# A planned single-core kernel: eight transfers in the planner's count, tile 2 on GpSimd's queue, and a new order

## The chip, the core and the metric

The kernel runs on one core of one Trainium2 chip. A core has TensorE (PE, matrix products and transposes), VectorE (DVE), ScalarE (ACT), GpSimd (POOL) and SyncE (SP, which here only issues DMAs), and 16 DMA engines that all issuers share. The metric is the device time of one execution in microseconds (us). Beside it the profiler gives the span of one execution, from its first to its last instruction.

## What is computed

Two batches of 1024 tokens with D = 2048 go through a quantized product with a context matrix and then through a routed low-rank layer. The parts of the reference that matter:

```python
def fake_quant(x, scale, zp):
    q = jnp.clip(jnp.round(x / s + z), QMIN, QMAX)
    return (q - z) * s
...
q1 = fake_quant(x1, x1_scale, x1_zp)
q2 = fake_quant(x2, x2_scale, x2_zp)
return jnp.matmul(q1, q2)
...
logits = jnp.einsum('bsd,ed->bse', x, route_w)
topk_v, topk_idx = jax.lax.top_k(logits, 1)
route_weight = jax.nn.one_hot(topk_idx[..., 0], E, dtype=logits.dtype) * topk_v
h = jnp.einsum('bsd,erd->bser', x, A)
wh = route_weight[..., None] * h
out = jnp.einsum('bser,eor->bso', wh, Bw) * SCALING
...
x = x + jnp.tanh(g_xattn[0]) * _L0_xattn_ref(_layernorm(x, axis=-1), ctx_4096, ...)
x = x + jnp.tanh(g_ffn[0]) * _L0_ffn_ref(_layernorm(x, axis=-1), L0_ffn_route_w, L0_ffn_A, L0_ffn_Bw)
```

x has shape (2, 1024, 2048), the context (2, 2048, 2048); there are E = 8 experts of rank 16. All inputs are float32.

## The kernel before

**Tiles and stages.** The 2048 tokens are 16 tiles of 128 (tiles 0 to 7 are batch 0, 8 to 15 batch 1). For each tile: load x (1 MB, L539), statistics, quantize (L623 on ScalarE or L632 on VectorE) and clamp (L629, L638), turn the 128 x 2048 result so that D lies on partitions, multiply by the quantized context (L704: 4 strips of 512 columns x 16 steps of K), evict with the corrections (L725, or L733 and L738), and then the feed-forward part (`ffn`). Statistics are four VectorE passes (L559, tiles in STATV) or two ScalarE passes (L577, then L587). The turn is a DMA transpose (L650, tiles in TURN) or 16 TensorE transposes (L660) with two copies (L524; with a tile in COPYV the second one is VectorE's). A row sum of the quantized tile (L675 on VectorE for SUMV, else L677 on ScalarE) goes into the correction.

**Context.** Each strip comes in four pieces of 1 MB (`strip`, load L432; a piece in FINE comes in two halves). It is scaled on ScalarE (L439) or VectorE (L450, pieces in VQ) and clamped (L446, L457). Column sums of a strip are 16 matmuls (L482) for strips in ONES, else VectorE additions and one matmul (L508). Four buffers hold raw pieces of batch 0, two those of batch 1. The strips of one batch serve groups of tiles: 0, 1, 2 together, then 3, 4, then 5, 6, 7 together; in batch 1 tiles 8, 9 together, then one by one.

**Feed-forward.** The new x must be turned once more, in float32, and multiplied by the 136 columns of `war`. Tiles in MOVE do it without TensorE transposes (`hidden_moved`): VectorE transposes 32 x 32 blocks (L760), DMAs move the blocks across partitions, ScalarE sorts (L800), TensorE multiplies (L804, 32 records). The DMAs are either 16 direct ones of 64 KB (`move`, L778) or, for tiles in VIA, one of 1 MB to DRAM (L770) and four back (`fetch`, L783). For tiles in TWO every second group of these DMAs is issued by ScalarE instead of SyncE. The other tiles use TensorE transposes (L822) with copies (L836) and products (L828). Then come a ScalarE square for the variance (L866), routing on VectorE (L877 to L886), a transpose (pw, L898) and copy (wht, L904), four output products (po, L911) with two banks, VectorE additions (L919), and the store (L932 on GpSimd's queue; the last tile's in four pieces on SyncE, L925).

**What sets the order.** No loop does. Every instruction, or a small group, is a `Task` with an engine, a cost, a rank, the tasks that it needs, and its buffers. `Plan.walk` goes through time: an engine that is free takes the task of lowest rank that is ready and has buffers. The resulting order is then issued on each engine, in order, and is fixed; only real waits (semaphores) apply on the chip. Ranks come from the position of a tile's strip in the sequence of matmul groups, less the entries of LEAD (statistics and quantization), XLEAD (x loads; XL0 for tiles 0 to 3), CTX and CQ (context), plus those of AFTER (feed-forward), SUM and COR (row sums, column sums). A DMA in the planner takes its bytes at 370 KB per us one after the other, plus 2.5 us and a slack; the number of DMAs in flight is not limited there.

**The first microseconds.** TensorE is kept busy by warm-up products (L356). SyncE's queue holds two scalars, half of tile 0, tile 1 in four pieces, the first context piece in halves, tile 2 in two pieces, three context pieces (the last in halves), tile 3, and the second strip; ScalarE's queue holds the other half of tile 0 and two scalars. GpSimd sets constants (L257 to L268) and later takes one power per tile (L609).

Of the kernel before, what the change touches and what calls it, by code (L numbers as in the profile page):

```python
# [17 lines left out]
P = 128  # L18
# [20 lines left out]
class Task:  # L39
    __slots__ = "eng cost rank fn needs bufs nbytes alone slack start end".split()  # L40


class Plan:
# [3 lines left out]

    def __init__(self, pools, kinds, hop, dma_rate, dma_delay):
        self.pools = pools
        self.kinds = kinds  # L50
        self.hop, self.rate, self.delay = hop, dma_rate, dma_delay
        self.tasks = []

    def add(self, eng, cost, rank, fn, needs=(), bufs=(), nbytes=0, alone=False, slack=0.0):

        t = Task()
        t.eng, t.cost, t.rank, t.fn, t.nbytes = eng, cost, rank, fn, nbytes
        t.alone, t.slack = alone, slack
        t.needs, t.bufs, t.start, t.end = list(needs), list(bufs), None, None
        for b in bufs:  # L60
            b.left += 1
        self.tasks.append(t)
        return t
# [10 lines left out]
    def walk(self):  # L74
# [8 lines left out]
        for w in waiting.values():  # L83
            w.sort(key=lambda t: t.rank)
        releases = []
        order = []
        now = 0.0
# [12 lines left out]
        while any(waiting.values()):  # L100
# [6 lines left out]
            for eng, w in waiting.items():  # L107
# [6 lines left out]
                for t in w:  # L114
                    at = self.ready_at(t)
                    if at is None:
                        continue
                    if at > now:
                        nxt.append(at)
                        continue  # L120
                    if t.alone and dma > now:
                        nxt.append(dma)
                        continue
                    if room(t):
                        pick = t
                        break
# [9 lines left out]
                if pick.nbytes:  # L136
                    dma = max(dma, now) + pick.nbytes / self.rate
                    pick.end = max(pick.end, dma) + self.delay + pick.slack
                for b in pick.bufs:
                    b.left -= 1  # L140
                    b.unit_end = max(getattr(b, "unit_end", 0.0), pick.end)
                    if not b.left:
                        releases.append((b.unit_end + self.hop, b))
# [13 lines left out]
def flamingo_gated_kernel(  # L157
# [42 lines left out]

    TURN = {4, 6, 7, 8, 11, 12, 13, 14, 15}
    MOVE = {3, 4, 8, 9, 10, 11, 12, 13, 14}
    pools = {"big": 10, "q2": 4, "half": 3, "q1t": 5, "wh": 2, "wht": 2, "bn": 3, "sel": 2, "away": 2}
    kinds = {k: (k, n) for k, n in pools.items()}
    kinds |= {"x": ("big", 6), "xl": ("big", 2), "st0": ("big", 4), "st1": ("big", 2), "ff": ("big", 4)}
    kinds |= {k: ("bank", n) for k, n in (("mm", 4), ("tp", 2), ("hl", 1), ("po", 2), ("cs", 1))}
    plan = Plan(pools | {"bank": 8}, kinds, hop=0.15, dma_rate=370e3, dma_delay=2.5)

# [77 lines left out]
    for tiles in sets:  # L286
# [5 lines left out]

    LATE = {4, 5, 6, 7}
    STATV = {0, 2, 3, 5, 13, 15}
    SUMV = {5, 6, 8, 14, 15}
    COPYV = {4, 5, 7, 9, 12, 14}
    ONES = {0}
    SUM = [2.5, 8.5, 8.5, 5.5, -1, 5.5, -1, 1.5, 5.5, 2.5, 3.5, 3.5, 8.5, 2.5, 0.5, 8.5]
    LEAD = [5, 7, 3, 5, 6, 3, 5, 14, 5, 8, 8, 12, 7, 7, 3, 14]
    XLEAD = [4, 4, 4, 4, 2, 1, 1, 8, 0, 6, 2, 1, 4, 3, 2, 2]  # L300
    XL0 = {0: -101, 1: -5.2, 2: -3.1, 3: -0.4}
    AFTER = [3.2, 6.2, 0.3, 1.2, -0.8, 0.7, 5.2, 5.2, 0.7, 0.7, 4.2, 6.2, 4.2, 4.2, 1.7, 3.2]
    CTX = [3, 1, 3, 4, 5, 4, 3, 2]
    COR = [1.5, 3.5, 0.5, 0.5, -0.5, 2.5, 2.5, 0.5]
    SLACK = 4.0
    VIA = {2, 3, 4, 5, 8, 9, 10, 12}
    TWO = {1, 3, 5, 6, 9, 10, 11, 12, 13, 14, 15}
    XL = {14, 15}
    PIECES = {0: 4, 1: 4, 2: 2, 3: 1}
    SPLIT = {0, 2}  # L310
    FINE = {0, 3, 4, 5}
    VQ = {0, 2, 3, 4, 9, 13, 14, 17, 20, 21, 41}
    CQ = {4: -1.8, 5: -1.1, 0: -1.1, 11: -1.0, 9: -0.2, 3: -0.1, 7: -0.6, 8: 1.1, 2: 0.2, 6: -0.9, 10: -1.5, 1: 0.7}
    SP, ACT, DVE, PE, POOL = "SP", "ACT", "DVE", "PE", "POOL"
# [8 lines left out]
    )  # L323
    t_raw = [
        add(SP, 0.9, -101.0, lambda: load_scalars(nc.sync, (0, 1)), nbytes=1, slack=3.0),
        add(ACT, 0.9, -100.9, lambda: load_scalars(nc.scalar, (2, 3)), nbytes=1, slack=3.0),
    ]
    t_gates = add(POOL, 1.1, -101, lambda: load_scalars(nc.gpsimd, (4, 5)), nbytes=1, slack=3.0)
    t_set = add(POOL, 2.0, -100, set_up_more)
# [196 lines left out]
    def tokens(t):  # L526
# [7 lines left out]
        loads = []  # L534
        for i in range(pieces):
            loads.append(
                add(
                    ACT if early and i % 2 else SP, 0.5, XL0.get(t, rank - XLEAD[t]),
                    lambda i=i: (nc.scalar if early and i % 2 else nc.sync).dma_start(  # L539
                        xx.ap()[:, ts(i, w)], x[b, ts(m, P), ts(i, w)]  # L540
                    ),
                    [t_ctx[1, NN - 1, NQ - 1]] if t in XL else [t_ctx[0, NN - 1, 1]] if t > 3 else [], [xx], nbytes=4 * P * w, slack=SLACK if t > 3 else 0.0 if t else 1.0,
                )
            )
# [203 lines left out]
    def hidden_moved(t, xx, hl, rank):  # L748
# [24 lines left out]
        for g in range(BPC):  # L773
# [8 lines left out]
            def fetch(g=g, queue=queue):  # L782
# [7 lines left out]
                if t in VIA  # L790
                else add(on, 2.6, rank - 0.5, move, turns, [turned, across], nbytes=4 * P * NC)
            )
# [49 lines left out]
    def ffn(t):  # L842
# [7 lines left out]
        p = (hidden_moved if t in MOVE else hidden)(t, xx, hl, rank)  # L850
        junk = flat("half", f"junk_{t}", F16, D)

# [5 lines left out]
        def inverse():  # L858
# [3 lines left out]

        a = add(DVE, 0.25, rank, mean, [t_x2[t, n] for n in range(NN)])
        a = add(
            ACT, 2.2, rank + 0.3,
            lambda: nc.scalar.activation(junk.ap(), xx.ap(), AF.Square, bias=nm, accum_out=sq),  # L866
            [a], [xx, junk],
        )
        t_r2 = add(DVE, 0.3, rank, inverse, [a])
        wh = buf("wh", f"wh_{t}", [P, E, R], F32)  # L870
# [3 lines left out]
        def route():  # L874
# [17 lines left out]

        a = add(DVE, 1.5, rank - 1, route, [p, t_r2, t_set], [hl, wh, sel_b])
        pw = buf("tp", f"pw_{t}", [P, NC], F32)
        wht = buf("wht", f"wht_{t}", [ER, P], F32)
        a = add(
            PE, 0.15, rank,
            lambda: nc.tensor.transpose(  # L898
# [4 lines left out]
        d = add(  # L903
            ACT, 0.28, rank - 1, lambda: nc.scalar.copy(wht.ap(), pw.ap()[:ER, :P]), [a], [pw, wht]  # L904
        )
        done = []
        for n in range(NN):
            po = buf("po", f"po_{t}_{n}", [P, NC], F32)
            a = add(
                PE, 0.87, rank,  # L910
                lambda n=n, po=po: nc.tensor.matmul(  # L911
# [8 lines left out]

            done.append(add(DVE, 0.75, rank - 0.5, finish, [a], [po, xx]))
            if end:
                add(
                    SP, 0.6, rank,
                    lambda n=n: nc.sync.dma_start(  # L925
# [4 lines left out]
        if not end:  # L930
            add(
                POOL, 0.6, rank, lambda: nc.gpsimd.dma_start(out[b, ts(m, P), :], xx.ap()),  # L932
                done, [xx], nbytes=4 * P * D,
            )
# [56 lines left out]
```

## Time and profile before

| quantity | value |
| --- | --- |
| median of three runs | 394.18 us (392.55 to 394.59) |
| the profiled execution: its own time | 394.16 us |
| the profiled execution: span | 392.4 us |
| granted TensorE clock, mean | 0.991 |
| main matmuls, L704 | 1024 records, 234.6 us |
| output products, L911 | 128 records, 60.5 us |
| hidden products, L804 and L828 | 512 records, 63.8 us |
| transposes of the quantized tiles, L660 | 112 records, 7.6 us |
| DMA traffic | 90.07 MB, mean 230 GB/s |
| transfers issued by SyncE, ScalarE | 69.80 MB, 4.20 MB |
| transfers issued by GpSimd | 15.73 MB |

A line of a group or of the timeline names line, engine, operation, output <- input, shapes and count; the bracket or the part behind the bar is the idle time of that engine just before and what ended it. A line of the stage table gives the stretch, the busy time and count of PE, PEld (weight loads), DVE, ACT and POOL, the granted clock, the busy share of the DMA engines and the GB/s. A float32 matmul leaves two records. Ends of matmuls are modelled, so lengths of single records overlap; the chain of waits shows the real pace. Some matmul records can be missing. Idle time of an engine that is not the bound costs nothing.

### The profile page before, as it was taken

The numbers are of one execution on the slowest core, as the hardware profiler recorded it, in microseconds if no ns is written. First come the engines' busy times: TensorE is split into PE (matmuls) and PEld (weight loads), VectorE is DVE, ScalarE is ACT, GpSimd is POOL, SyncE is SP. The second block draws the span as 40 slices with busy tenths as digits, with TensorE's granted clock in tenths as the row PEclk, the third lists the DMA queues.
The fourth block names the chain that finished last, engine by engine and source line by source line (L and its number), as shares of the span: only waits on it lengthen the run. The fifth ranks groups of instructions, "written<-read, shape, count | busy, mean of one in ns | idle before, by whom it ended". The sixth has DMA issues, their size and how long they took to land.

```text
span 392.4 us, 5340 instructions
## 1 busy us (share of the span) xinstructions
PE 374.7 (96%) x1969; PEld 216.5 (55%) x1969; DVE 305.1 (78%) x711; ACT 233.0 (59%) x225; POOL 23.6 (6%) x52
## 2 busy tenths in 40 slices
PE   4689999999999999999999999999999999999994
PEld 4544445657654654654756674444646455666671
DVE  3699999997977398794699659999779777676553
ACT  1799995699624536889979895656545042402140
POOL 3010000010001000010010010001010000000000
PEclk9879999999999999999999999999999999999999
DMA  6999999805548928998798478356366727767222
GB/s 211 342 396 388 387 372 377 322 0 109 214 150 320 226 109 254 395 406 261 241 333 309 146 270 280 109 160 143 74 198 178 208 115 214 215 209 211 119 106 108
DMA packets 50658, 90.07 MB, mean 230 GB/s; under 512 B 21320, under 2 KB 23368, under 8 KB 46152
## 3 DMA queue, kind: packets, MB, share of 16 engines
q1 hardware_dynamic: 45812, 69.80, 54.3%
q0 software_dynamic: 2224, 15.73, 10.0%
q10 hardware_dynamic: 2596, 4.20, 4.7%
q8 instruction: 15, 0.25, 0.3%
q14 instruction: 11, 0.09, 0.1%
HBM read 58.79 MB, written 23.07 MB: 209 GB/s over the span
## 4 chain that ended last, share of the span: by engine, by line
PE 75%; DMA 13%; DVE 6%; ACT 2%; SPq 1%; issue 1%; ACTq 0%
PE mm L704 45%; PE po L911 12%; PE hl L804 8%; PE hl L828 6%; DMA across<-away 4%; DMA st<-in_ctx_dram 3%; DMA away<-turned 3%; PE px L822 3%; DMA across<-turned 2%; DMA x<-in_x_dram 1%; PE pq L660 1%; ACT turned L800 1%; DVE turned L760 1%; DVE x L733 1%; DVE q L450 1%
## 5 line engine op out<-in xcount | busy, mean ns | idle before, releaser
L704 PE MATMUL mm<-q,q1t 128*128 128x512 f16 x1024 | 234.6, 380 | 4.1 <-ACT q1t L524 2.7
L704 PEld LDWEIGHTS <-q1t 128*128 128x128 f16 x1024 | 100.0, 98 | 124.3 <-issue 15.6
L439 ACT ACTIVATE q<-st,raw,rs 128x2048 int16<-128x2048 f32 (+1 forms) x30 | 57.3, 1919 | 13.3 <-PE mm L704 9.0
L911 PE MATMUL po<-wb,wht 128*128 128x512 f32 x128 | 60.5, 594 | 0.4 <-ACT wht L904 0.4
L919 DVE SCALAR_TENSOR_TENSOR x<-po,th,x 128x512 f32<-128x512 f32 x64 | 47.2, 748 | 15.8 <-PE po L911 13.0
L866 ACT ACTIVATE junk<-x,mine 128x2048 f16<-128x2048 f32 x16 | 32.1, 2005 | 21.3 <-DVE mine L854 21.2
L733 DVE SCALAR_TENSOR_TENSOR x<-mm,sc,x 128x512 f32<-128x512 f32 x48 | 35.2, 744 | 10.2 <-PE mm L704 10.1
L904 ACT COPY wht<-pw 128x128 f32<-128x128 f32 x16 | 4.2, 264 | 57.6 <-PE pw L898 41.7
L623 ACT ACTIVATE q<-x,mine 128x2048 int16<-128x2048 f32 (+1 forms) x16 | 31.7, 1984 | 9.9 <-DVE mine L603 7.1
L804 PEld LDWEIGHTS hl<-war,turned 128*128 128x128 f32 x288 | 34.6, 190 | 5.0 <-ACT turned L800 2.8
L804 PE MATMUL hl<-war,turned 128*128 128x136 f32 x288 | 35.3, 280 | 1.1 <-ACT turned L800 1.1
L738 DVE SCALAR_TENSOR_TENSOR x<-x,mine,corr 128x512 f32<-128x512 f32 x48 | 35.2, 746 | 1.6 <-ACT corr L515 0.8
L911 PEld LDWEIGHTS po<-wb,wht 128*128 128x128 f32 x128 | 23.4, 190 | 19.9 <-issue 13.2
L828 PE MATMUL hl<-war,xt 128*128 128x136 f32 x224 | 28.5, 280 | 0.4 <-ACT xt L836 0.4
L828 PEld LDWEIGHTS hl<-war,xt 128*128 128x128 f32 x224 | 27.4, 190 | 1.9 <-ACT xt L836 0.9
L587 ACT ACTIVATE q<-x,mine 128x2048 f16<-128x2048 f32 x10 | 20.0, 1997 | 8.4 <-DVE mine L582 8.4
L800 ACT COPY turned<-across 128x1024 f32<-128x1024 f32 x18 | 17.9, 1041 | 9.6 <-DMA across<-away 5.6
L760 DVE STREAM_TRANSPOSE turned<-x 128x512 f32<-128x512 f32 x36 | 22.9, 683 | 0.2 <-DMA across<-away 0.2
L836 ACT COPY xt<-px 128x512 f32<-128x512 f32 x28 | 15.7, 583 | 10.7 <-PE px L822 10.7
L559 DVE BATCH_NORM_STATS2 bn<-x 128x6 f32<-128x512 f32 x24 | 15.3, 682 | 8.2 <-DMA x<-in_x_dram 8.2
L932 POOL DMA_DIRECT2D out_dram<-x x15 | 8.7, 583 | 204.5 <-DVE x L919 156.8
L677 ACT ACTIVATE q<-q 128x2048 f16<-128x2048 f16 x11 | 20.9, 1904 | 0.0
(93 smaller groups left out, 318.9 us busy)
## 6 DMA issues: line engine op xcount, KB each, us to landing
st<-in_ctx_dram SPq DMA_DIRECT2D x28, 1024.0 KB, 10.8
out_dram<-x POOLq DMA_DIRECT2D x15, 1024.0 KB, 5.0
x<-in_x_dram SPq DMA_DIRECT2D x13, 1024.0 KB, 4.8
away<-turned SPq DMA_DIRECT2D x6, 1024.0 KB, 3.9
st<-in_ctx_dram SPq DMA_DIRECT2D x8, 512.0 KB, 12.9
across<-away SPq DMA_DIRECT2D x16, 256.0 KB, 6.3
across<-away ACTq DMA_DIRECT2D x8, 256.0 KB, 6.1
x<-in_x_dram SPq DMA_DIRECT2D x6, 256.0 KB, 5.0
```

The lines of the kernel that those rows point to most:

```text
L439: nc.scalar.activation(part.bitcast(I16), st.ap().rearrange("p (k n) -> p k n", k=QK)[:, ts(h, n)], AF.Relu, bias=z2, scale=rs2,)
L623: nc.scalar.activation(qb.ap()[:, ts(h, hw)].bitcast(I16), xx.ap()[:, ts(h, hw)], AF.Relu, bias=nb, scale=a)
L704: lambda k=k: nc.tensor.matmul(acc.ap(), qt.ap()[:, k, :], qb.ap()[:, k, :], start=(k == 0), stop=(k == KC - 1)),
L733: lambda: nc.vector.scalar_tensor_tensor(xs(), acc.ap(), c, xs(), ALU.mult, ALU.add),
L738: lambda: nc.vector.scalar_tensor_tensor(xs(), xs(), rs_[t], corr[:, ts(s, NC)], ALU.add, ALU.add, accum_out=ss),
L760: nc.vector.transpose(turned.ap().rearrange("p (g k i) -> p k g i", i=BLK, k=KC)[:, ts(n, BPC)], xx.ap()[:, ts(n, NC)].rearrange("p (k g j ...
L800: nc.scalar.copy(o[:, ts(h, KC // H)], i[:, ts(h, KC // H)])
L804: nc.tensor.matmul(hl.ap()[:, : ER + E], turned.ap()[:, ts(k, P)], war[:, k, :], start=(k == 0), stop=(k == KC - 1),)
L828: nc.tensor.matmul(hl.ap()[:, : ER + E], xt.ap()[:, ts(k, P)], war[:, k, :], start=(k == 0), stop=(k == KC - 1),)
L866: lambda: nc.scalar.activation(junk.ap(), xx.ap(), AF.Square, bias=nm, accum_out=sq),
L911: lambda n=n, po=po: nc.tensor.matmul(po.ap(), wht.ap(), wb[:, ts(n, NC)], start=True, stop=True),
L919: nc.vector.scalar_tensor_tensor(xs, po.ap(), gf, xs, ALU.mult, ALU.add)
```

## The change

The planner gets a limit: with eight transfers (counted in parts, for SyncE and ScalarE together and for GpSimd apart) under way, the next waits for the eighth last to land. Tasks that issue several transfers say so. Tile 2's x load moves to GpSimd's queue (XPOOL). The second half of the feed-forward part (pw, wht, po, finish, store) gets a rank of its own, later by POR[t]. An alternative for the second variance on VectorE is added, but its set BN2 is empty. All tables of the order are replaced.

```diff
@@ Plan.walk
         releases = []
+        landed = {}
...
+                    under_way = landed.get(t.eng == "POOL", [])
+                    if t.nbytes and len(under_way) >= self.most and under_way[-self.most] > now:
+                        nxt.append(under_way[-self.most])
+                        continue
                     if room(t):
...
                     pick.end = max(pick.end, dma) + self.delay + pick.slack
+                    landed.setdefault(eng == "POOL", []).extend([pick.end] * pick.parts)
@@ flamingo_gated_kernel
-    TURN = {4, 6, 7, 8, 11, 12, 13, 14, 15}
-    MOVE = {3, 4, 8, 9, 10, 11, 12, 13, 14}
+    TURN = {4, 6, 11, 12, 13, 14, 15}
+    MOVE = {3, 4, 6, 8, 10, 11, 12, 13, 14}
...
-    plan = Plan(pools | {"bank": 8}, kinds, hop=0.15, dma_rate=370e3, dma_delay=2.5)
+    plan = Plan(pools | {"bank": 8}, kinds, hop=0.15, dma_rate=370e3, dma_delay=2.5, most=8)
...
-    LATE = {4, 5, 6, 7}
-    STATV = {0, 2, 3, 5, 13, 15}
-    SUMV = {5, 6, 8, 14, 15}
-    COPYV = {4, 5, 7, 9, 12, 14}
+    LATE = {4, 5, 6, 7, 10, 15}
+    STATV = {0, 1, 3, 5, 12, 13, 14}
+    SUMV = {2, 5, 6, 8, 12, 14}
+    COPYV = {0, 3, 4, 5, 7, 9, 14}
     ONES = {0}
-    SUM = [2.5, 8.5, 8.5, 5.5, -1, 5.5, -1, 1.5, 5.5, 2.5, 3.5, 3.5, 8.5, 2.5, 0.5, 8.5]
-    LEAD = [5, 7, 3, 5, 6, 3, 5, 14, 5, 8, 8, 12, 7, 7, 3, 14]
-    XLEAD = [4, 4, 4, 4, 2, 1, 1, 8, 0, 6, 2, 1, 4, 3, 2, 2]
-    XL0 = {0: -101, 1: -5.2, 2: -3.1, 3: -0.4}
-    AFTER = [3.2, 6.2, 0.3, 1.2, -0.8, 0.7, 5.2, 5.2, 0.7, 0.7, 4.2, 6.2, 4.2, 4.2, 1.7, 3.2]
-    CTX = [3, 1, 3, 4, 5, 4, 3, 2]
-    COR = [1.5, 3.5, 0.5, 0.5, -0.5, 2.5, 2.5, 0.5]
+    SUM = [0.5, 8.5, 2.5, 1.5, -1, 1.5, 1.5, 2.5, 5.5, 2.5, 8.5, 1.5, 8.5, 8.5, 1.5, 8.5]
+    LEAD = [6, 14, 10, 8, 6, 5, 8, 14, 5, 5, 8, 14, 4, 6, 4, 6]
+    XLEAD = [4, 4, 4, 4, 0, 4, 3, 10, 2, 10, 3, 1, 4, 2, 6, 0]
+    XL0 = {0: -101, 1: 2.2, 2: -4.0, 3: 4.4}
+    AFTER = [1.2, 6.2, 2.2, 2.2, 0.3, -0.8, 4.2, 5.2, -0.8, 3.2, 6.2, 6.2, 4.2, 1.7, 5.2, 2.2]
+    CTX = [8, 6, 5, 5, 5, 5, 4, 3]
+    COR = [2.5, 1.5, 7.5, 0.5, 1.5, 1.5, -0.5, 0.5]
     SLACK = 4.0
-    VIA = {2, 3, 4, 5, 8, 9, 10, 12}
-    TWO = {1, 3, 5, 6, 9, 10, 11, 12, 13, 14, 15}
-    XL = {14, 15}
-    PIECES = {0: 4, 1: 4, 2: 2, 3: 1}
-    SPLIT = {0, 2}
-    FINE = {0, 3, 4, 5}
-    VQ = {0, 2, 3, 4, 9, 13, 14, 17, 20, 21, 41}
-    CQ = {4: -1.8, 5: -1.1, 0: -1.1, 11: -1.0, 9: -0.2, 3: -0.1, 7: -0.6, 8: 1.1, 2: 0.2, 6: -0.9, 10: -1.5, 1: 0.7}
+    VIA = {0, 2, 3, 5, 9, 12, 14}
+    TWO = {0, 1, 4, 5, 7, 9, 11, 13, 15}
+    XL = {15}
+    PIECES = {0: 4, 1: 4, 2: 2, 3: 4}
+    SPLIT = {0}
+    FINE = {3, 6}
+    VQ = {0, 4, 5, 6, 8, 9, 15, 17, 19, 21, 27, 33, 39, 44, 51}
+    XPOOL = {2}
+    POR = [0, 0, 1.5, 1, 0, 2, 1.5, 0, 1.5, 0.5, 0, 0.5, 0, 1, 2, 1.5]
+    BN2 = set()
+    CQ = {4: -1.2, 5: -1.6, 0: 1.2, 11: -1.3, 9: -0.9, 3: 0.6, 7: 0.8, 8: -0.9, 2: 1.3, 6: -2.0, 10: -1.1, 1: 1.3}
@@ tokens
+            queue = (
+                (ACT, nc.scalar) if early and i % 2 else (POOL, nc.gpsimd) if t in XPOOL else (SP, nc.sync)
+            )
...
-                    ACT if early and i % 2 else SP, 0.5, XL0.get(t, rank - XLEAD[t]),
+                    queue[0], 0.5, XL0.get(t, rank - XLEAD[t]),
@@ hidden_moved
-                else add(on, 2.6, rank - 0.5, move, turns, [turned, across], nbytes=4 * P * NC)
+                else add(on, 2.4, rank - 0.5, move, turns, [turned, across], nbytes=4 * P * NC, parts=4)
@@ ffn
+        behind = rank + POR[t]
...
-            PE, 0.15, rank,
+            PE, 0.15, behind,
...
-            ACT, 0.28, rank - 1, lambda: nc.scalar.copy(wht.ap(), pw.ap()[:ER, :P]), [a], [pw, wht]
+            ACT, 0.28, behind - 1, lambda: nc.scalar.copy(wht.ap(), pw.ap()[:ER, :P]), [a], [pw, wht]
...
-                PE, 0.87, rank,
+                PE, 0.87, behind,
...
-            done.append(add(DVE, 0.75, rank - 0.5, finish, [a], [po, xx]))
+            done.append(add(DVE, 0.75, behind - 0.5, finish, [a], [po, xx]))
```

Entries of VQ count twice the piece's number, plus one for a second half; odd entries of pieces that come whole have no effect, nor have entries of COPYV for tiles in TURN or of VIA for tiles outside MOVE. LATE tiles take their corrections in one wide VectorE pass (L716) ahead of the matmuls' eviction (L725) instead of one pass per strip behind it (L738).

## The prediction

> **What bounds the kernel now.** I read the engine totals first, then the slices, then a table by stages.
>
> ```profile
> PE 374.7 (96%) x1969; PEld 216.5 (55%) x1969; DVE 305.1 (78%) x711; ACT 233.0 (59%) x225; POOL 23.6 (6%) x52
> ...
> PE   4689999999999999999999999999999999999994
> ```
>
> TensorE is the bound: in the slices it is full but for the first three and the last. The stage table (columns: stretch, busy time of each engine, granted clock, DMA share, GB/s) says how full:
>
> ```profile
> 21.00:28.50 7.50, 7.35 (x38) 3.26 (x36) 7.17 (x16) 7.50 (x8) 1.81 (x1) 0.78 1.04 400
> 28.50:62.00 33.50, 33.28 (x179) 16.16 (x180) 31.69 (x59) 32.39 (x25) 0.89 (x1) 1.00 1.06 374
> 62.00:130.00 68.00, 67.63 (x359) 39.59 (x357) 59.31 (x148) 40.34 (x45) 4.33 (x7) 1.00 0.61 210
> 130.00:200.00 70.00, 69.06 (x377) 39.23 (x375) 51.55 (x118) 53.88 (x46) 4.19 (x5) 1.00 0.81 275
> 200.00:300.00 100.00, 100.00 (x510) 54.15 (x508) 84.11 (x201) 69.22 (x66) 5.01 (x9) 1.00 0.63 198
> 300.00:373.30 73.30, 73.11 (x392) 45.86 (x391) 51.46 (x120) 15.99 (x21) 2.69 (x5) 1.00 0.60 180
> ```
>
> From 28.5 to 373.3 TensorE stands only 0.22 + 0.37 + 0.94 + 0 + 0.19 = 1.7 us. And "busy" is real there: the chain of waits has nine main matmuls in 1.94 us, 0.216 each, everywhere. So a new order can win only (a) before 28.5, (b) those 1.7 us, (c) behind 373.3; and added TensorE work costs its full time.
>
> (a) The start, TensorE's timeline first (start, length, idle before), then ScalarE's:
>
> ```profile
> 14.87 1.07 PE L660 MATMUL pq<-idh,q 128*128 128x128 f16 x16 [0.55 <-DVE q L629]
> 18.42 1.03 PE L704 MATMUL mm<-q,q1t 128*128 128x512 f16 x2 [2.48 <-ACT q1t L524]
> 20.88 1.01 PE L704 MATMUL mm<-q,q1t 128*128 128x512 f16 x2 [1.42 <-DVE q L446]
> ```
> ```profile
> 11.22 1.91 ACT L577 ACTIVATE q<-x 128x2048 f16<-128x2048 f32 x1 [1.44 <-DMA x<-in_x_dram]
> ...
> 13.13 1.23 ACT L623 ACTIVATE q<-x,mine 128x1024 int16<-128x1024 f32 x1
> 14.26 1.99 ACT L587 ACTIVATE q<-x,mine 128x2048 f16<-128x2048 f32 x1
> ...
> 16.25 1.23 ACT L439 ACTIVATE q<-st,raw,rs 128x1024 int16<-128x1024 f32 x1
> 17.38 0.99 ACT L524 COPY q1t<-pq 128x1024 f16<-128x1024 f16 x1
> ```
>
> (ScalarE's first line is tile 1's statistics, waiting for tile 1's load; tile 0's own quantization and copy stand behind it.) By 28.5 TensorE has done 12 main matmuls, 12 column sums and 16 transposes: 24 x 0.216 + 0.9 = 6.1 us of work at full clock. It had half the clock from 17.7 to 24.2. The second piece of context (1 MB) was issued at 9.65 and landed at 21.0, since tile 1 (four pieces), tile 2 and the first context piece go before it, and because the early transfers are slow:
>
> ```profile
> 1.39 5.99 SPq L539 DMA_DIRECT2D x<-in_x_dram  x6
> ```
> ```profile
> 2.00:16.00 14.00, 9.29 (x54) 8.64 (x52) 7.22 (x24) 6.47 (x7) 2.45 (x15) 1.00 0.88 280
> ...
> 16.00:30.00 14.00, 10.00 (x53) 4.59 (x54) 12.30 (x32) 11.79 (x13) 2.37 (x2) 0.76 1.04 398
> ```
>
> SyncE takes 6 us for six issues of 0.43 us, because with eight in flight it waits for landings; meanwhile 280 GB/s move, where 398 do later.
>
> (c) The end. The last tile's product runs to 382.2, then VectorE routes, and nothing is left for TensorE:
>
> ```profile
> 383.55 0.33 PE L898 MATMUL pw<-idf,wh 128*128 128x128 f32 x1 [1.37 <-DVE wh L886]
> 384.29 3.70 PE L911 MATMUL po<-wb,wht 128*128 128x512 f32 x8 [0.41 <-ACT wht L904]
> ```
>
> 1.8 us of idle; the 4.3 us behind 388.1 (last VectorE pass and store) stay.
>
> **The parts and their prices.**
>
> *Start.* By the new ranks SyncE issues tile 0, then the first strip's four context pieces (five transfers), then tile 1's four, then the second strip. Tile 2 goes by GpSimd, ready there when its constants are set (4.04); its two issues last 0.58 each, and GpSimd's next work, a 0.56 us power for tile 0, came at 9.5: no delay. Tile 2 takes tile 1's old place (its statistics now on ScalarE), tile 1 takes tile 2's (on VectorE). Context pieces 1 and 2 go into the issue slots that tile 1's four pieces had (4.2 to 7.1), so they are behind 3 MB instead of 4 and 5. At 390 GB/s from 5 us on, pieces 0 to 3 land near 12.8, 15.5, 18.2 and 21, against 21.0 for piece 1 before.
> The unknown is when tile 2 lands, as ScalarE's in-order queue should stop at its statistics before tile 0's quantization. Before shows no load on GpSimd; the nearest rows are its stores of the same 1 MB:
>
> ```profile
> out_dram<-x POOLq DMA_DIRECT2D x15, 1024.0 KB, 5.0
> ```
> ```profile
> out_dram<-x POOLq DMA_DIRECT2D x1, 1024.0 KB, 10.6
> ```
>
> 5.0 us is the median, 10.6 the store at 167.9, beside a full SyncE queue, 7.7 one beside a half-full queue. From 4.6 that is 9.6, 12.3 or 15.2. I take 12.1. Then ScalarE: 1.9 + 1.2 + 2.0 + 1.0 = 6.0 with overlap (the 1.2 us context piece in between is now VectorE's), first matmul at 18.1. From there TensorE always has work: piece 0 is ready at about 15, piece 1 at 20.9 (ScalarE 2.1, clamp 0.7), the others by 24.3, tile 2 by 26. Half clock lasts, as before, 3.3 us of steady work: 1.65 us of work by 21.4, then 7.1 by 28.5, together 8.75 against 6.1: **-2.6 us**. Landing at 9.6: first matmul near 16, starved between pieces, but at full clock: -4. Landing at 15.2: first matmul at 21.2, work 1.65 + 4.0: **+0.4**.
>
> The page "TensorE: Matmul & The Clock Gate" of the Trainium skill (HAM oscillation; PE-mode transpose) has the clock fall after about 3.4 us without matmuls and says transposes do not count as such. Here the last warm-up ended at 14.3 and the clock fell near 17.7, in spite of transposes to 15.9. By that rule a tile 2 that lands before about 11.7 keeps the clock, worth up to 1.65 us more. "DMA: Bandwidth & Descriptors" (Issuing engines are not separate DMA queues) speaks against the GpSimd load: all issuers share the 16 engines and only issue time is saved; by it the 12.1 would lean to 15.2, and the sum to +3 on mine.
>
> *Transposes.* Tiles 7 and 8 leave the DMA transpose (9 tiles to 7): 32 more transposes on a full TensorE, 16 take 0.89 us in the chain: **+1.8 us**. Moves of the hidden state stay nine (6 in, 9 out), so no change in px work; main, product and output matmuls stay.
>
> *End.* Ranks now set tile 14's output (66.2) behind tile 15's product (65.2) and before tile 15's output (66.7). Its 3.4 us cover route 15, but finishes queue behind that route on VectorE and only two output banks exist, so some 0.4 of idle stays: **-1.4 us**. That tile 15 is LATE brings its last eviction 0.75 us forward, which tile 14's product hides. (0 for the end if tile 14's move through DRAM is late: 5.6 + 7.6 + 1.05 in the chain's worst, under the 13.8 us of tile 15's matmuls and 7 of tile 13's).
>
> *VectorE and ScalarE.* One tile more of statistics (+3.0 VectorE, -4.3 ScalarE), one row sum (+2.4, -2.1), copies 2 to 5 on VectorE (+2.1; ScalarE 12 to 13, +1.0), context scalings (-0.8, +0.5), tile 2's split gone (-0.8, +0.9), tiles 10 and 15 in LATE (one pass of 2.35 us, L716, for four of 0.75 + 0.08, L738, less four reads of 0.08: -0.6 each): VectorE +4.7 to 310 of 392, ScalarE -4. I count 0, since both have room after 62 (VectorE 59 of 68, 52 of 70). If it loses this cover, up to +2; where a stall ends sooner, -1.
>
> *SyncE.* Direct moves go from three tiles to six: 24 to 72 issues there, 48 x 0.59 = 28 us more, less 3 stores and 4 fetches (2.7). Two DMA transposes that stop the queue go. Tiles 6, 8 and 10 have all 16 issues on SyncE: 9.4 us in a row, against 4.7 when shared. The way through DRAM took 13.3 us in the chain, the direct one 10, so alone on SyncE 14.7: about equal. I take 0 for the mid holes; bounds -1.7 (none left) and +6.
>
> Sum against the profiled execution (394.16; span 392.4; the median of the runs is 394.18, so the same): 394.16 - 2.6 + 1.8 - 1.4 + 0 = **392.0**.
>
> **Rivals.**
> *Given back* (394.6): tile 2 lands after 15 (break-even at 14.8), or ScalarE and VectorE, 97 and 95% busy from 28.5 to 62, cannot deliver earlier. Start 0 to +0.4, end -1.4, transposes +1.8: 394.2 to 395.0. For it: those shares; against: 2 us of idle ScalarE from 18.4 to 20.6 that work would fill.
> *SyncE late* (398, the other side): the order on TensorE is fixed, so a product whose move is late stops it. Place: L804 behind the copy L800 behind the last of 16 issues. If tiles 6, 8 and 10 come 2 us late each, +6: 394.16 - 2.6 + 1.8 - 1.4 + 6 = 398. It decides against the forecast's gain when the new holes pass 2.2 us, and gives a measurable loss past 4.1. For it: SyncE stood behind other waits at such moves for up to 9.9 us; before's 0.86 and 0.19 us at L804 are of this kind. Against: the cost in the code, 2.4 for four issues, is the measured 4 x 0.59.
> *All comes* (388.9): landing near 9.6 (-4), holes gone (-1.7), end and transposes as above: 394.16 - 4 - 1.7 - 1.4 + 1.8.
>
> **Chances.** Forecast 0.42, given back 0.20, SyncE late 0.26, all comes 0.12. A measurement tells 0.5% (392.2 and 396.2 against 394.18). The forecast lies at that edge: 0.31 faster, 0.11 same; given back 0.17 same, 0.03 slower; late 0.26 slower; all comes 0.12 faster. Faster 0.43, same 0.28, slower 0.29. Range: from just under "all comes" to "late", 388 to 398.
>
> **What would show it.** Right: second context piece landed by 16, first matmul by 18.5 with no gap over 0.5 us behind it, 144 transposes at L660, no 1.4 us gap before the last pw, idle between 28.5 and the last main matmul at most 2 us. Wrong: ScalarE idle past 13 before tile 2's L577, gaps at L804 over 1 us, or gaps at the main matmul between 30 and 62.

## The result, and the profile after

The changed kernel takes **393.58 us** (median of 22 runs, 391.98 to 395.90), the kernel before in the same comparison 394.02 (22 runs, 392.38 to 395.21). The ratio is **0.9997, interval 0.9978 to 1.0016**: no difference. The forecast was 392.0. The profiled execution after took 393.32 us, 0.84 less than the one before.

| | before | after |
| --- | --- | --- |
| profiled execution, span | 392.4 | 391.4 |
| first main matmul begins | 18.42 | 21.94 |
| TensorE idle, 28.5 to the last main matmuls | 1.7 | 0.1 |
| last output product ends | 388.0 | 384.95 |
| from there to the end of the span | 4.4 | 6.4 |

The totals, the slices and the stage table of the profile after (columns as before):

```profile
PE 375.3 (96%) x2001; PEld 219.0 (56%) x2001; DVE 307.8 (79%) x709; ACT 228.6 (58%) x219; POOL 22.9 (6%) x54
...
PE   5689999999999999999999999999999999999993
```
```profile
28.50:62.00 33.50, 33.49 (x182) 16.30 (x181) 32.52 (x60) 31.64 (x23) 0.55 (x1) 1.00 1.05 378
62.00:130.00 68.00, 68.00 (x373) 40.63 (x372) 54.42 (x133) 41.48 (x47) 3.75 (x6) 1.00 0.48 178
130.00:200.00 70.00, 69.97 (x396) 39.99 (x394) 60.14 (x125) 49.84 (x43) 3.84 (x5) 1.00 0.73 236
200.00:300.00 100.00, 99.92 (x514) 56.33 (x513) 85.64 (x206) 61.15 (x60) 6.18 (x11) 1.00 0.67 216
300.00:370.00 70.00, 70.00 (x364) 41.54 (x363) 47.72 (x116) 24.27 (x27) 2.17 (x4) 1.00 0.54 159
```

Second column less third: between 28.5 and 370 TensorE stands 0.1 us in all. In this execution the middle is full, so what was won must have been lost at one of the two ends.

The end, TensorE's timeline of after (output products are now L945, pw is L932):

```profile
377.01 0.27 PE L932 MATMUL pw<-idf,wh 128*128 128x128 f32 x1
377.70 1.98 PE L945 MATMUL po<-wb,wht 128*128 128x512 f32 x4 [0.41 <-ACT wht L938]
379.52 0.27 PE L932 MATMUL pw<-idf,wh 128*128 128x128 f32 x1
379.63 5.32 PE L945 MATMUL po<-wb,wht 128*128 128x512 f32 x12
```

The wait of 1.37 us before the last pw is gone, as foreseen; one of 0.41 is left. TensorE ends 3.0 us sooner than before, the span only 1.0. Where did 2 us go? VectorE's last pass ends 0.78 us behind the last product in both kernels (388.77 before; 381.55 + 4.18 = 385.73 after). The rest is stores. The DMA view of the last stretch (376 to 393), line by line output <- input, queue, count, KB each, median us from issue to landing; before, then after:

```profile
out_dram<-x POOLq DMA_DIRECT2D x1, 1024.0 KB, 4.1
out_dram<-x SPq DMA_DIRECT2D x4, 256.0 KB, 2.4
```
```profile
out_dram<-x POOLq DMA_DIRECT2D x1, 1024.0 KB, 4.2
out_dram<-x SPq DMA_DIRECT2D x4, 256.0 KB, 4.6
```

And the issues, GpSimd's and SyncE's timelines, before and then after:

```profile
379.12 0.53 POOL L932 DMA_DIRECT2D out_dram<-x  x1 [10.40 <-DVE x L919]
```
```profile
386.23 2.91 SPq L925 DMA_DIRECT2D out_dram<-x  x4
```
```profile
382.59 0.53 POOL L966 DMA_DIRECT2D out_dram<-x  x1 [23.27 <-DVE x L953]
```
```profile
383.18 3.85 SPq L959 DMA_DIRECT2D out_dram<-x  x4
```

Tile 14's store, 1 MB, waits for all four additions of tile 14. The new order put these right before tile 15's, so the store leaves 0.6 us before tile 15's first piece, and the four pieces need 4.6 us instead of 2.4. (Before, tile 14's store left at 379.12, 7 us before the first piece.)

The start, timelines of TensorE and ScalarE after (transposes L674, column sums L493, main matmuls L718; tile 2's statistics L591):

```profile
17.75 1.03 PE L674 MATMUL pq<-idh,q 128*128 128x128 f16 x8 [3.67 <-DVE q L643]
18.58 1.91 PE L493 MATMUL cs<-q,ones 128*128 128x512 f16 x4
```
```profile
13.19 1.91 ACT L591 ACTIVATE q<-x 128x2048 f16<-128x2048 f32 x1 [4.83 <-DMA x<-in_x_dram]
...
18.22 2.08 ACT L450 ACTIVATE q<-st,raw,rs 128x2048 int16<-128x2048 f32 x1
20.20 0.98 ACT L535 COPY q1t<-pq 128x1024 f16<-128x1024 f16 x1
```

Tile 2 landed at about 13.1, not 12.1. ScalarE then took a context piece (18.22) before tile 0's copy (20.20), which the prediction had left out, so main matmuls begin at 21.94 and not at 18.1; column sums run from 18.58. From tile 0's own transposes to 28.5 TensorE has done 12 column sums, 18 main matmuls and 16 transposes of the next tile: 30 x 0.216 + 0.9 = 7.4 us of work, against 6.1 before and the 8.75 that were forecast (both counted in the same way).

### The profile page after: what moved, and what is told of

Same layout as the page of the kernel before. It is cut to its first block, busy times and chain, and to the rows that moved or that the text cites. A ratio compares the mean times of both kernels' runs of the same rounds, so it can differ in the third digit from the quotient of the medians.

```text
span 391.4 us, 5431 instructions
## 1 busy us (share of the span) xinstructions
PE 375.3 (96%) x2001; PEld 219.0 (56%) x2001; DVE 307.8 (79%) x709; ACT 228.6 (58%) x219; POOL 22.9 (6%) x54
## 4 chain that ended last, share of the span: by engine, by line
PE 91%; ACT 3%; DMA 2%; issue 1%; POOL 1%; DVE 0%; POOLq 0%; ACTq 0%
PE mm L718 56%; PE po L945 14%; PE hl L818 9%; PE hl L842 7%; PE px L836 3%; DMA x<-in_x_dram 2%; PE pq L674 2%; ACT q L637 1%; ACT q L450 1%; ACT q L601 1%; ACT q1t L535 1%; ACT q L691 0%; PE pw L932 0%; PE cs L519 0%; POOL row L265 0%
## 5 line engine op out<-in xcount | busy, mean ns | idle before, releaser
L718 PE MATMUL mm<-q,q1t 128*128 128x512 f16 x1024 | 233.3, 379 | 0.7 <-ACT q1t L535 0.7
L718 PEld LDWEIGHTS <-q1t 128*128 128x128 f16 x1024 | 99.8, 98 | 119.1 <-issue 10.9
L945 PE MATMUL po<-wb,wht 128*128 128x512 f32 x128 | 60.6, 595 | 0.4 <-ACT wht L938 0.4
L637 ACT ACTIVATE q<-x,mine 128x2048 int16<-128x2048 f32 (+1 forms) x16 | 32.6, 2040 | 24.2 <-DVE mine L617 14.8
L818 PEld LDWEIGHTS hl<-war,turned 128*128 128x128 f32 x288 | 34.8, 190 | 2.7 <-issue 1.1
L818 PE MATMUL hl<-war,turned 128*128 128x136 f32 x288 | 35.3, 280 | 0.1
L945 PEld LDWEIGHTS po<-wb,wht 128*128 128x128 f32 x128 | 23.4, 190 | 21.3 <-issue 14.9
L747 DVE SCALAR_TENSOR_TENSOR x<-mm,sc,x 128x512 f32<-128x512 f32 x40 | 29.4, 744 | 4.1 <-PE mm L718 3.7
L752 DVE SCALAR_TENSOR_TENSOR x<-x,mine,corr 128x512 f32<-128x512 f32 x40 | 29.4, 746 | 1.1 <-DVE x L747 0.5
L739 DVE SCALAR_TENSOR_TENSOR x<-mm,sc,x 128x512 f32<-128x512 f32 x24 | 17.6, 746 | 12.4 <-PE mm L718 12.3
L691 ACT ACTIVATE q<-q 128x2048 f16<-128x2048 f16 x10 | 19.1, 1907 | 9.1 <-DMA q1t<-q 9.1
L774 DVE STREAM_TRANSPOSE turned<-x 128x512 f32<-128x512 f32 x36 | 24.1, 693 | 0.0
L457 DVE TENSOR_SCALAR q<-q 128x2048 f16<-128x2048 int16 (+1 forms) x29 | 19.1, 662 | 3.5 <-ACT q L450 3.5
L573 DVE BATCH_NORM_STATS2 bn<-x 128x6 f32<-128x512 f32 x28 | 17.9, 681 | 4.8 <-DMA x<-in_x_dram 4.8
```

The costliest lines, as they stand in the source:

```text
L457: nc.vector.tensor_scalar(part, part.bitcast(I16), QMAX, MID, ALU.min, ALU.subtract)
L637: nc.scalar.activation(qb.ap()[:, ts(h, hw)].bitcast(I16), xx.ap()[:, ts(h, hw)], AF.Relu, bias=nb, scale=a)
L718: lambda k=k: nc.tensor.matmul(acc.ap(), qt.ap()[:, k, :], qb.ap()[:, k, :], start=(k == 0), stop=(k == KC - 1)),
L747: lambda: nc.vector.scalar_tensor_tensor(xs(), acc.ap(), c, xs(), ALU.mult, ALU.add),
L752: lambda: nc.vector.scalar_tensor_tensor(xs(), xs(), rs_[t], corr[:, ts(s, NC)], ALU.add, ALU.add, accum_out=ss),
L774: nc.vector.transpose(turned.ap().rearrange("p (g k i) -> p k g i", i=BLK, k=KC)[:, ts(n, BPC)], xx.ap()[:, ts(n, NC)].rearrange("p (k g j ...
```

## The experiments

Ratios are to the kernel before, run beside each kernel on the same chip, with 95% intervals. "Span" is that of the profiled execution. The groups e1 to e4, e5 to e8, e9 to e12 and e13 to e15 ran at different times, not all on one chip; medians are best compared within a group, ratios across groups.

| run | what | median | ratio | span |
| --- | --- | --- | --- | --- |
| e1_strips | after, tile 14's store in four | 391.43 | 0.9967 (0.9933 to 1.0001) | 388.7 |
| e2_tile2_sync | after, tile 2 by SyncE | 393.30 | 1.0008 (0.9984 to 1.0032) | 390.4 |
| e3_both | e1 and e2 | 390.42 | 0.9944 (0.9914 to 0.9973) | 388.7 |
| e4_por14 | after, tile 14's output early again | 392.74 | 1.0007 (0.9978 to 1.0035) | 391.8 |
| e5_no_limit | after, no count of transfers | 404.95 | 1.0268 (1.0230 to 1.0306) | 400.9 |
| e6_before_limit | before, planner counts eight | 403.46 | 1.0239 (1.0191 to 1.0287) | 402.2 |
| e7_turn78 | after, tiles 7, 8 by DMA transpose | 393.59 | 1.0014 (0.9984 to 1.0045) | 391.3 |
| e8_before_por | before, tile 14's output late | 392.63 | 0.9971 (0.9952 to 0.9991) | 390.9 |
| e9_after | after again | 394.19 | 1.0015 (0.9989 to 1.0041) | 393.9 |
| e10_both | e3 again | 391.57 | 0.9935 (0.9920 to 0.9949) | 390.6 |
| e11_before_por_strips | e8, store in four | 390.74 | 0.9921 (0.9907 to 0.9935) | 388.7 |
| e12_quant0_first | e3, tile 0's quantize first | 391.32 | 0.9939 (0.9916 to 0.9961) | 389.2 |
| e13_after_swap | after, a load behind tile 3's move | 393.57 | 1.0009 (0.9988 to 1.0030) | 391.8 |
| e14_both_swap | e3 with e13 | 391.93 | 0.9953 (0.9932 to 0.9974) | 390.1 |
| e15_before_end_again | e11 again | 391.18 | 0.9949 (0.9927 to 0.9970) | 389.4 |

**The end: is it the store?** e1 splits tile 14's store; each piece goes as soon as its addition is done.

```diff
-        if not end:
+        if t == NT - 2:
+            for n in range(NN):
+                add(
+                    POOL, 0.6, behind,
+                    lambda n=n: nc.gpsimd.dma_start(
+                        out[b, ts(m, P), ts(n, NC)], xx.ap()[:, ts(n, NC)]
+                    ),
+                    [done[n]], [xx], nbytes=4 * P * NC,
+                )
+        elif not end:
...
```

> The changed kernel with tile 14's store in four pieces of 256 KB, each behind its own addition, in place of one of 1 MB behind all four; everything else stands in the same order. Store theory (tile 14's 1 MB store, issued at 382.6, shares the DMA engines with tile 15's four pieces, which land in 4.6 us instead of 2.4): the pieces of tile 14 start near 379.6, tile 15's pieces land in about 2.5 us again, and from the last output product to the end of the span it is 4.4 us as in the kernel before, not 6.4: about -2.0 us, 391.5. Rival (the end is longer for another reason, such as the order of the last additions): the distance stays near 6.4 us and the time near 393.5.

The DMA view of e1's last stretch:

```profile
out_dram<-x POOLq DMA_DIRECT2D x4, 256.0 KB, 2.7
out_dram<-x SPq DMA_DIRECT2D x4, 256.0 KB, 2.9
```

The last pieces land in 2.9 us, and the span ends 4.7 us behind the last output product (388.7 - 384.0), not 6.4: of the 2.0 us, about 1.8 come back. That the collision of stores costs them is shown in the profile. In the runs' times e1 alone is not told from the kernel before (its interval reaches 1.0001); e10 below, beside e9, is.

e4 undoes the other half: `POR[14]` from 2 to 0, so tile 14's output no longer goes between tile 15's product and tile 15's output.

> The changed kernel with POR[14] at 0 instead of 2: tile 14's output products go before tile 15's hidden product again, and nothing covers the last routing. Store theory: the idle of TensorE before the last pw comes back (about 1.4 to 1.8 us), but tile 14's store is out some 3.5 us earlier and tile 15's pieces land in 2.4 us again (-2.1): together 0 to -0.7 us against the changed kernel. Rival (only TensorE's idle counts): +1.4 us or more, 395.

TensorE's timeline of e4, then its DMA view of the last stretch:

```profile
382.91 0.30 PE L932 MATMUL pw<-idf,wh 128*128 128x128 f32 x1 [1.46 <-DVE wh L919]
383.62 3.70 PE L945 MATMUL po<-wb,wht 128*128 128x512 f32 x8 [0.41 <-ACT wht L938]
```
```profile
out_dram<-x SPq DMA_DIRECT2D x4, 256.0 KB, 2.5
```

The idle time is back and the collision is gone; the time is that of after. So in the changed kernel the edit at the end moves 1.4 us from TensorE to the stores, and by itself is worth nothing.

e8 puts this edit alone into the kernel before, e11 adds the split store.

```diff
+    POR = {14: 5.8, 15: 0.5}
...
+        behind = rank + POR.get(t, 0)
...
```

As in the changed kernel, `behind` is then the rank of pw, copy, po, additions and store.

> The kernel before with the second half of tiles 14 and 15 apart (POR 5.8 and 0.5: tile 14's output behind tile 15's hidden product, as in the changed kernel); the order is otherwise the old one. Store theory: TensorE's idle before the last pw goes (-1.4 to -1.8 us at the last output product), but tile 14's 1 MB store meets tile 15's pieces, the way from the last output product to the end grows from 4.4 to about 6.4 us, so in sum 0 to +0.6 us against the kernel before. Rival (TensorE's idle alone counts): -1.4 us or more, and 4.4 us stay.

> The kernel before with tile 14's output behind tile 15's hidden product (as e8) and tile 14's store in four pieces; nothing else of the change. Store theory: TensorE's idle at the end goes and the stores do not collide: -1.8 us from the idle, 4.4 us behind the last output product, so about 391.6, and that is what the changed kernel would have had from its ranks apart alone. Rival (the end of the old order has no room for it): 393 or more.

Tile 14's hidden product, the same point of the order in all three, on TensorE's timelines of before, e8 and e11:

```profile
366.93 3.87 PE L804 MATMUL hl<-war,turned 128*128 128x136 f32 x32
```
```profile
365.55 3.87 PE L805 MATMUL hl<-war,turned 128*128 128x136 f32 x32
```
```profile
365.04 3.87 PE L805 MATMUL hl<-war,turned 128*128 128x136 f32 x32
```

From there to the end of the span: 392.4 - 366.93 = 25.47 before, 390.9 - 365.55 = 25.35 in e8, 388.7 - 365.04 = 23.66 in e11. At the end, then, the edit alone is worth 0.1 and with the split 1.8, as the theory has it. The stores agree: in e8 tile 15's pieces need 4.5 us and the span ends 6.4 behind the last output product, in e11 2.9 and 4.7. Yet the spans are 1.5 and 3.7 shorter: the other 1.4 and 1.9 us lie ahead of that point, where the instructions and their order are the same as before. Most of it, 0.9 and 1.1 us, is there already at the first hidden product (76.56 before, 75.67 and 75.46): the wait of 1.42 us for scaled context near 20.9, which the profile before has, is in neither. The kernel before itself ran from 392.38 to 395.21, so one profiled execution of each cannot say more; in the medians beside them e8 is 0.9 us and e11 3.2 us under the kernel before. Why e8 gains at all in its runs stays open. e15 repeated e11:

> The kernel of e11 once more, beside these: the kernel before, with the new end and the store in four pieces alone. By its terms 1.8 us under the kernel before; if the first measurement holds, 3.2 us under it (near 390.7).

391.18, 0.9949: a gain of 0.3 to 0.7%, a little smaller than in e11; by the medians 1.9 us, near the 1.8 that the end explains. The kernel before with its end mended is thus as good as the whole change with the end mended (e3, e10), and both beat both kernels.

**The start.** e2 takes tile 2 back to SyncE, the planned order untouched.

```diff
-                (ACT, nc.scalar) if early and i % 2 else (POOL, nc.gpsimd) if t in XPOOL else (SP, nc.sync)
+                (ACT, nc.scalar) if early and i % 2 else (POOL, nc.sync) if t in XPOOL else (SP, nc.sync)
```

> The changed kernel with the two pieces of tile 2's load issued by SyncE, at the same place of the order, in place of GpSimd; no other instruction moves. Theory (on GpSimd's queue tile 2 shares the engines with context pieces 0 and 1, lands at 13.1, and ScalarE stands 4.8 us before its statistics): on SyncE it stands ahead of the context, lands near 9.5, ScalarE starts L591 there, tile 0's second half of transposes comes near 14 instead of 17.8, and the first main matmul near 18.5 instead of 21.9; context pieces 0 to 3 land about as before, as the bytes ahead of them are the same. If TensorE is the bound from there on, -2 us or more at the last output product. Rival 1 (the context sets the start): first products earlier, but waits for pieces 1 to 3 take it back, 0 to -0.5 us. Rival 2 (GpSimd's queue is a gain, since SyncE's eight are taken): tile 2's pieces fill SyncE's eight, context piece 0 goes out after 5 instead of 4.0, later pieces up to 1 us later, 0 to +1 us.

> Both edits of this set, tile 14's store in four pieces and tile 2 on SyncE. If store theory and queue theory are both right, they add up, since one is at each end of the span: -4 us against the changed kernel, near 389.5. If only one is right, near 391.5; if neither, near 393.5.

ScalarE's timeline of e2:

```profile
11.56 1.91 ACT L591 ACTIVATE q<-x 128x2048 f16<-128x2048 f32 x1 [3.09 <-DMA x<-in_x_dram]
```

Tile 2 comes 1.6 us sooner than by GpSimd's queue, and the last output product ends 0.9 us sooner in the profile; in the runs' times the difference is not told from nothing. With both edits (e3) the median is 390.42, between the 389.5 expected if both theories held and the 391.5 if one did. e12 asks whether ScalarE's order around tile 2 matters: in e3's order, tile 0's quantization and clamp of the first half go before tile 2's statistics.

> The kernel of e10 with one move in the fixed order: ScalarE quantizes tile 0's first half, and VectorE clamps it, before tile 2's statistics, not behind them. Theory (tile 0's turn waits for tile 2's landing through ScalarE's queue): TensorE's wait of 2.7 us before the second half of tile 0's transposes goes, the first column sums start up to 0.8 us earlier, and the end comes 0.3 to 0.8 us earlier. Rival (the start is set by context piece 1 behind ScalarE's full queue): that wait goes, but TensorE waits as much longer before the second column sums, and the time stays.

TensorE's timeline of e12 (transposes are L676 there):

```profile
12.61 1.06 PE L676 MATMUL pq<-idh,q 128*128 128x128 f16 x16
15.75 1.02 PE L493 MATMUL cs<-q,ones 128*128 128x512 f16 x4 [2.08 <-DVE q L468]
18.93 1.87 PE L493 MATMUL cs<-q,ones 128*128 128x512 f16 x4 [2.16 <-DVE q L457]
```

The wait inside tile 0's transposes (4.05 us in e10, the same kernel without this move, and 2.70 in e3) is gone, and two waits of 2.1 us for scaled context stand in its place; the time stays (391.32 beside e10's 391.57). Tile 2 was not what the start depends on: context pieces behind ScalarE's and VectorE's full queues are.

**The transposes.** e7 gives tiles 7 and 8 back to the DMA transpose (`TURN = {4, 6, 7, 8, 11, ...}`); the planner orders anew.

> The changed kernel with tiles 7 and 8 in TURN again: DMA transposes in place of 32 TensorE transposes and four copies; the plan is the same up to the middle of the first batch, then worked out anew. Price theory (added TensorE work costs its full time): TensorE's work falls by 32 x 0.056 = 1.8 us and the last output product ends 1.8 us earlier, unless the two DMA transposes, which want no other transfer ahead of them, open holes on TensorE; idle between 28.5 and 370 then shows how much, and I expect 0.5 to 1 us, so -0.8 to -1.3. Rival (the transposes stood in idle time of TensorE anyway): 0. Rival (the DMA transposes stop SyncE's queue): idle over 2 us, +0.5 us or more.

Its stage table:

```profile
62.00:130.00 68.00, 67.70 (x359) 39.91 (x358) 56.70 (x134) 39.85 (x45) 3.31 (x6) 1.00 0.57 195
130.00:200.00 70.00, 69.50 (x384) 39.77 (x383) 59.90 (x132) 52.28 (x44) 4.39 (x6) 1.00 0.76 239
...
300.00:370.00 70.00, 69.05 (x355) 40.42 (x354) 48.14 (x119) 24.55 (x25) 2.16 (x4) 1.00 0.53 158
```

1.8 us less work, and 0.30 + 0.50 + 0.95 = 1.75 us of idle back; after had 0.1. TensorE's waits of e7 from 28.5 on (total, times, longest):

```profile
PE po L945 <- ACT wht L938: 1.1, 3, 0.4
PE pw L932 <- DVE wh L919: 0.5, 1, 0.5
PE hl L818 <- ACT turned L814: 0.5, 1, 0.5
```

None of them ends at a DMA transpose: 0.4 of the first line is the wait at the very end that after has too, the rest are waits for routing, for its copy and for a moved hidden state. So work and idle time balance here, but that the DMA transposes themselves made the holes is not shown: the planner ordered everything behind them anew, and the wait at L818 comes and goes without them too (see the spread, below).

**The planner's count.** e5 lifts it (`most=10000`) with the new tables; e6 puts the count (with `parts` and 2.4 for 2.6) into the planner of before with the old tables.

> The changed kernel with its new tables, planned without the limit of eight (most=10000), so that the order is worked out anew under the old belief; GpSimd's load and the second half's ranks stay. The changed kernel has 0.1 us of idle on TensorE between 28.5 and 370, the kernel before 1.7. Limit theory (the holes are gone because the planner now knows that transfers wait for the eighth last): idle between 28.5 and 370 comes back to 1.5 us or more, and the time to 395 or more. Rival (the tables were searched with that planner, and any other plan from them is worse for no reason of its own): idle of 3 us or more, not at waits for DMAs alone. Rival (the limit matters little): under 0.7 us, time within 1 us of the changed kernel's 393.6.

> The kernel before with its old tables, planned with the limit of eight, parts counted and the direct move at 2.4; nothing else of the change. Limit theory: the idle of TensorE between 28.5 and 370 falls from 1.7 to under 0.7 us, -1 us or more against the kernel before. Rival (old tables fit the old planner): the new order has more idle than 1.7 us, and the time is 395 or more.

Stage tables of e5, then of e6:

```profile
28.50:62.00 33.50, 29.39 (x165) 14.80 (x164) 30.34 (x57) 33.34 (x24) 1.09 (x2) 0.95 1.06 378
```
```profile
130.00:200.00 70.00, 66.51 (x363) 38.81 (x361) 48.56 (x110) 42.72 (x36) 2.82 (x5) 0.98 0.71 219
200.00:300.00 100.00, 96.70 (x501) 53.78 (x500) 83.78 (x195) 70.43 (x66) 5.80 (x9) 1.00 0.78 235
```

Each crossing is 2.4 to 2.7% slower (four runs each), in different places: 4.1 us of idle in one wait near the start in e5, with 3.3 us more at two moved hidden products, and 6.8 in the middle in e6. So the count by itself does not remove holes; as far as these two runs show, each set of tables fits the planner with which it was searched.

**The spread.** Half of after's 22 runs lie from 391.98 to 393.42, half from 393.73 to 395.90; the kernel before spreads nearly as widely (392.38 to 395.21). e9 looks again.

> The changed kernel once more, beside the next three on one chip, so that they can be compared with it: 393.3 to 393.9.

> The changed kernel with tile 14's store in four pieces and tile 2 on SyncE (as e3), with more rounds. Store theory: -2.0 us against the changed kernel from the store, and what tile 2's earlier landing gives, 0 to -1: 390.5 to 391.5. Rival (the first measurement was a lucky draw of starts): 392.5 or more.

e10's six runs lie from 390.50 to 392.40; the slowest is its profiled execution, with a hole of 1.81 us at L818. e9's 12 runs lie at 392.17 to 393.45 and 394.93 to 396.92; its profiled execution took 395.72. TensorE's and SyncE's timelines of e9, each followed by the same stretch of after:

```profile
137.67 5.64 PE L818 MATMUL hl<-war,turned 128*128 128x136 f32 x32 [1.89 <-ACT turned L814]
```
```profile
136.51 3.97 PE L818 MATMUL hl<-war,turned 128*128 128x136 f32 x32
```
```profile
118.73 0.34 SPq L553 DMA_DIRECT2D x<-in_x_dram  x1
119.96 0.33 SPq L784 DMA_DIRECT2D away<-turned  x1
```
```profile
118.55 0.34 SPq L553 DMA_DIRECT2D x<-in_x_dram  x1
120.66 0.33 SPq L784 DMA_DIRECT2D away<-turned  x1
126.60 2.57 SPq L797 DMA_DIRECT2D across<-away  x4
```

In e9 tile 3's way to DRAM (L784) starts 1.23 us behind a load of 1 MB instead of 2.1, and lands in 8.3 us instead of 5.8; the hidden product then waits 1.89 us and runs 1.67 us longer, together some 3.5. Eight traces have the load ahead of the move, and they line up: where it left 1.8 to 2.1 us earlier (after, e1, e2, e3, e12) TensorE's wait is 0 to 0.5 us, at 1.3 (e4) it is 1.1, at 1.2 and 1.1 (e9, e10) 1.9 and 1.8. The move starts when VectorE has turned the tile; the load starts 0.14 us after a 1 MB store on GpSimd's queue has landed, and SyncE's wait view names that store. It needed 5.1 us in after (113.30 to 118.41) and 6.0 in e9 (112.61 to 118.59). To test the cause, e13 puts that load behind tile 3's move in SyncE's order; e14 does so in e3.

```diff
+    i = order.index(t_away[3])
+    j = max(k for k in range(i) if order[k].eng == SP)
...
+    order.insert(i, order.pop(j))
```

> The changed kernel with one exchange in SyncE's order: the x load that stands ahead of tile 3's way to DRAM (L784) goes behind it; nothing else moves. Theory (that load, when it is issued late, shares the engines with the way to DRAM, and tile 3's product, which TensorE's order has fixed, waits up to 1.9 us and then runs at half clock): the wait at L818 near 136 is gone in the trace, the way to DRAM lands in under 6 us, single runs stay in one group of 391.9 to 393.4, median near 392.5. Rival (the two groups come from the start): the groups stay, median 393.3 to 394.2. Rival (the load is then late itself): a wait near tile 7's or 8's first product, 394 or more.

> The same exchange in the kernel of e10 (tile 14's store in four pieces, tile 2 on SyncE). Theory: one group near 390.3 to 390.7, -1 us against e10's 391.6. Rivals as for e13: 391 to 392 with the two groups, or 392 and more.

Timelines of SyncE and TensorE in e13 (lines one further on):

```profile
124.97 2.93 SPq L798 DMA_DIRECT2D across<-away  x4
```
```profile
137.13 3.97 PE L819 MATMUL hl<-war,turned 128*128 128x136 f32 x32 [1.34 <-ACT turned L815]
```

The runs now lie in one stretch (392.78 to 395.01), and the move goes sooner (fetches at 124.97). But the load now meets the four fetches, and a hole of 1.34 us stands there; the median is the same. e14 gains nothing either (391.93; e10 had 391.57), with a wait of 1.3 us at the same place. So the move is sooner without the load ahead of it, as thought; that the exchange would remove the hole was wrong, and that this load alone makes the hole in e9 is likely from the eight traces but not shown by an edit.

## Why the prediction was wrong

**The step that failed** is the one it did not work out: "the 4.3 us behind 388.1 (last VectorE pass and store) stay". They became 6.4. The edit that fills TensorE's gap delays tile 14's additions, so tile 14's 1 MB store leaves 3.5 us later (379.12 to 382.59), beside tile 15's pieces. The prediction priced the moved output on TensorE and did not follow its store. e1 and e11 show it with the collision removed, e4 with the edit undone, e8 with the edit alone in the old order. The second step that failed is the size of the start, half of what was forecast.

Against the profiled execution the sum is now 394.16 - 1.3 (start) + 1.8 (transposes) - 1.4 (end idle) - 1.6 (middle) + 2.0 (stores) = 393.7, where 393.32 was measured; the other 0.3 us are not accounted for.

- *Start*, -2.6 forecast, -1.3 by the same count of work. Tile 2 was 1 us later than taken, and a context piece of 2.1 us stood between on ScalarE. The prediction named the wrong gate: e2 brings tile 2 sooner and e12 takes the wait away, and neither changes the time measurably. Its own signs said so: main matmuls began at 21.94, past its mark of 18.5, with a wait of 0.72 us behind them, and ScalarE stood until 13.19, past its mark of 13. The clock before fell at about 17.5, a little sooner than the 17.7 that was read (granted 0.96 from 17 to 17.5, 0.50 from 17.5 to 18).
- *Transposes*, +1.8: right as a price; e7 takes it out and has 1.75 us of holes in its place.
- *End idle*, -1.4: right to the tenth, and e4 shows its loss when undone.
- *Middle*, 0 forecast, -1.6 in this execution, which is luck as much as order: in e9, the same kernel, a hole of 1.89 us and a slower product behind it take it back.
- *Rivals*. "Given back" (394.6) comes nearest to the time, by other means than it named: not a tile 2 past 15, but the stores. (Its parts add up to 394.6 to 395.0; the lower bound of 394.2 was a slip.) "SyncE late" had the right line (a product waiting behind the sorting copy behind a DMA), but the tile is 3, whose way goes through DRAM and meets a load; the 16 issues in a row of tiles 6, 8 and 10 stopped nothing for long.
- *Range.* The time lay in 388 to 398, but a gain of 2.2 us was forecast and no difference came, an outcome to which the prediction gave 0.28.

Open: why e8 is faster than the kernel before in its runs, when its end is not; what moves context and loads by about 1 us at the start from one execution to the next; and why the store ahead of the load at 118.5 needs 5.1 us in one and 6.0 in another.

## What to carry to other kernels

When work of the last but one tile is pushed behind the last tile's to fill a gap of the bound engine, look at which stores are then in flight together: here the gap was won only when the last store was not joined by a bigger one, and splitting that bigger one gave the gain back. A planner and the tables searched with it belong together: here changing the planner under either set of tables cost 2.4 and 2.7%. And where an order already leaves TensorE 0.5% of idle time, edits can just exchange one wait for another (e12, e13); mend one place and measure it alone (e11) before searching everything anew.

## What the runs showed of the hardware

Pieces of 256 KB landed in 2.4 to 2.5 us by themselves (before, e4), 2.8 to 2.9 beside four like them (e1, e3, e10, e11), and 4.5 to 4.6 behind a store of 1 MB from another queue (after, e2, e8). A move of 1 MB to DRAM took 5.8 us 2.1 us behind a load of 1 MB (after), 7.3 at 1.3 (e4) and 8.3 at 1.2 and 1.1 (e9, e10).

The clock: after a wait of 3.67 us inside tile 0's transposes the profile after had 0.53 from 17 to 18 and 0.51 from 18 to 20.5. e2 has a wait of 3.68 at the same place and kept full clock; e1 lost it with a wait of 3.17 (0.50 from 18 to 20). The stage-table rows of after, then of e2:

```profile
18.00:20.50 2.50, 2.49 (x12) 1.19 (x10) 1.79 (x7) 2.50 (x4) 0.55 (x1) 0.51 1.05 387
```
```profile
16.00:21.00 5.00, 2.54 (x17) 1.34 (x18) 4.14 (x10) 4.61 (x5) 0.55 (x1) 1.00 1.04 383
```

Likewise e9's hidden product behind the wait of 1.89 us: in its stretch the granted clock was 0.70, and 0.3 of 5.6 us is the 1.67 by which it runs longer. In e10 a wait of 1.81 at the same place left full clock. Rows of e9, then of e10:

```profile
137.60:143.20 5.60, 5.53 (x33) 5.51 (x34) 0.69 (x1) 2.96 (x3) 0.00 (x0) 0.70 0.50 113
```
```profile
138.00:142.00 4.00, 3.94 (x33) 3.90 (x34) 0.69 (x1) 2.95 (x3) 0.00 (x0) 1.00 0.73 161
```

The page "TensorE: Matmul & The Clock Gate" of the Trainium skill (What's actually happening) has the clock follow a window of about 3.4 us that runs freely, so that a change depends on where in it the work falls. Two outcomes for one gap of 3.7 us agree with that; the waits of 3.17 us in e1 and 1.89 in e9, behind which the clock dropped too, are shorter than that window, and no run here says why.
